# A two-layer attention network: attn3's row sums by quarters of the columns, sums and steps moved, and the last store on another queue

## The chip, the cores and the metric

The kernel runs on one core of one Trainium2 chip. The metric is the device time of one execution in microseconds, taken as the median of several runs. The core has four compute engines with instruction streams of their own: PE (TensorE, matrix products), DVE (VectorE), ACT (ScalarE) and POOL (GpSimd). SP (SyncE) issues most of the transfers.

## The reference

The input x has two images of 512 channels and 64 x 32 positions, that is 2048 tokens each, in f32. Two layers follow one another.

```python
# layer 0: full attention, 8 heads of 64, S = 2048 tokens
attn = softmax(q k^T / 8);  x = x + (attn v) Wout + bout
# layer 1: layer norm, then Nystroem attention with 256 landmarks
qL, kL = means of q, k over groups of 8 tokens
attn1 = softmax(q kL^T)      # 2048 x 256
attn2 = softmax(qL kL^T)     # 256 x 256
attn3 = softmax(qL k^T)      # 256 x 2048
out = attn1 @ (pinv(attn2) @ (attn3 @ v))   # pinv: 6 iterations
out = out + depthwise convolution of v over 33 tokens
t = t + out Wout + bout
# then layer norm, and two matrices, the first from 4-bit indices
t = t + (norm(t) W_lora^T) W^T
```

All of it is computed in f32, and the softmaxes are written without a subtraction of the maximum: exponentials are summed, and the product with the values is multiplied by the reciprocal of the sums.

## The kernel before, in words

Heads are worked on in pairs, with one head in partitions 0 to 63 and the other in 64 to 127. There are four pairs for each of the two images. A path called `fast_path` runs where a bound computed from q and k says that the exponentials are safe; the other path is not taken here.

The program order of PE, DVE, ACT and POOL is the order in which the code issues the instructions. Only the transfers on SP's queue are placed by a scheduler, in one order for that queue; each waits in that order for its own inputs and buffers.

**Layer 0** ends with a loop over four blocks of 512 tokens (L1820 and the lines after it). It weaves three generators: the output projection of the next block (`more_out`), the layer norm of this one (`norm`), and the second layer's projections and Gram products for the pairs of the image done before (`more`). `advance(gens, n)` makes n steps of a list of generators. In the norm, a mean and a variance over the channels are products with a constant matrix (`mean_n` L990 and `var_n` L1006), and the square root on ACT needs a table load (L1008). The projections are `pp` (L1245), copied by ACT (L1248); the landmark softmax `X` is normalised on DVE (L1299), and Gram products `pr` of it (L1313) are copied by ACT (L1320) and stored.

**Layer 1** has a main loop over the list `todo`, the four pairs of image 1 and then those of image 0, named 1_1_0 to 1_0_3. While the pseudo-inverse of pair n is iterated on PE (`pinv`, products pa and pb L1538), hooks fill PE's time with work of its neighbours. The hook `chunk(c)` runs after each of the first five iterations, c = 0 to 4, and `last(i)`, i = 0 to 5, between the products of the sixth, which is applied to the values alone (`wp`, L1513).

- In `chunk(c)`, c below 4, stands a quarter of attn3 of pair n+1: scores (L1367), exponentials (L1376), and the products with v, `attn3_values` (L1388, tensor tiles 128*64). Among them stands a quarter of attn1 of pair n-1: scores (L1595), the addition of the two halves (L1604), values (L1611), then `attn1_sums` (products with ones, L779, tiles 128*32, and an ACT copy L1619) and `attn1_inverse` (reciprocal L1624, and a spread). `attn1_end(c-1)` multiplies on DVE (L1631) and adds on POOL (L1632).
- `spread` (L790) is eight transfers on SP from SBUF to SBUF: the sums were made in 32 partitions for each half of the columns, and the reciprocals are copied to all 64 partitions of the head.
- In `chunk(4)` begins `landmarks_values` of pair n+1 (L1407): row sums `rs3` of attn3 by products with ones (L1412, tiles 128*64, every partition of a head gets the sum), an ACT copy (L1421), a reciprocal (L1422) and the multiply (L1423) on DVE, and the loads of X (L1427). After it comes the depthwise convolution of pair n+1, `cv` (L1465), in four blocks of 512 tokens, each copied by ACT.
- For pairs 1_0_1 and 1_0_2 there is no whole tile for the convolution's result. ACT copies each block into a row (L1477) and SP stores that row to `o_fd` (L1478). `row_of` gives rows from a pool of three buffers, which the spreads of attn1 use too.
- After the convolution, PE transposes M (`tp_M`, L1528), ACT copies it (L1529), and `wp` (L1513) multiplies with it. In `last(1)` the generator of `landmarks_values` goes on: transposes `tp` (L1431), a copy Y (L1433) and the loads of A (L1439).

For the first pair, `second_of_first` does the same steps ahead of the loop, with a unit of projections between each two of them.

**The end.** Image 0 is finished by blocks: output projection, norm, the last product `fp_g` (L1694), and for each 128 channels `rest` (multiply L1683, add L1684, store L1685 on SP). The last 128 channels of the last block are done in two halves of 256 columns.

Of the kernel before, what the change touches and what calls it, by code (L numbers as in the profile page):

```python
# [13 lines left out]
ALU = mybir.AluOpType  # L14
AX = mybir.AxisListType

P = 128
# [3 lines left out]
HEADS, D = 8, 64  # L21
NPAIR = HEADS // 2
TB = 512
NTB = S // TB
NST = S // P
LM, POOL = 256, S // 256
# [627 lines left out]
Q = P // 4  # L654
# [9 lines left out]
def fast_path(  # L664
# [35 lines left out]
    nc = tc.nc  # L700
# [27 lines left out]
    def chunked(ap):  # L728
        return ap.rearrange("(k p) n -> p k n", p=P)
# [40 lines left out]
    csum = const.tile([P, B * NPAIR, 4], F32, name="csum1")  # L770


    def sums_of(rs, acc):


        for h in range(2):
            for j in range(2):
                lo = h * D + j * Q
                nc.tensor.matmul(  # L779
                    rs[lo : lo + Q, :LM], lhsT=ones[:, :Q], rhs=acc[:, h, j * LM : (j + 1) * LM],  # L780
                    start=True, stop=True,
                )

    def spread(dst, few):

        for h in range(2):
            for to in range(2):
                for j in range(2):
                    lo, src = h * D + to * Q, h * D + j * Q
                    nc.sync.dma_start(dst[lo : lo + Q, j * LM : (j + 1) * LM], few[src : src + Q, :])  # L790


    def advance(gens, n=1):
# [420 lines left out]
    class Pair:  # L1214
# [192 lines left out]
        def landmarks_values(self):  # L1407

            rs = bank(f"rs3_{self.name}")
            for j in range(2):  # L1410
                for h in range(2):
                    nc.tensor.matmul(  # L1412
                        rs[h * D : (h + 1) * D, :LM],
                        lhsT=ones,
                        rhs=self.acc3[:, h, j * LM : (j + 1) * LM],
                        start=j == 0,
                        stop=j == 1,
                    )
            rinv = self.acc3[:, 0, :]
            yT = rinv[:, LM:]  # L1420
            nc.scalar.copy(rinv[:, :LM], rs[:, :LM])  # L1421
            nc.vector.reciprocal(rinv[:, :LM], rinv[:, :LM])  # L1422
            nc.vector.tensor_tensor(yT, self.av3[:, :LM], rinv[:, :LM], ALU.mult)  # L1423
            X = exps(f"X2_{self.name}").rearrange("p a b -> p (a b)").rearrange("p (h k n) -> p h k n", h=2, k=2)
            self.X = [X[:, h] for h in range(2)]
            for h in range(2):
                nc.sync.dma_start(self.X[h], X_d[self.b, self.hp, h])  # L1427
            yield
            tp = bank(f"tp_{self.name}")
            for t in range(2):  # L1430
                nc.tensor.transpose(tp[:, t * P : (t + 1) * P], yT[:, t * P : (t + 1) * P], ident)  # L1431
            self.Y = lmpool.tile([P, 2, P], F32, tag="Y", name=f"Y_{self.name}")
            nc.scalar.copy(self.Y, tp[:, :LM].rearrange("p (t n) -> p t n", t=2))  # L1433
            A = zpool.tile([P, 2, 2, LM + 1], F32, tag="Q", name=f"A_{self.name}")
            self.A = [A[:, h] for h in range(2)]
            for h in range(2):
                for t in range(2):
                    cols = slice(t * P, LM)
                    nc.sync.dma_start(self.A[h][:, t, cols], A_d[self.b, self.hp, h][:, t, cols])  # L1439
            yield  # L1440
# [193 lines left out]
    class Finish1:  # L1634
# [42 lines left out]
        def map_units(self, bank_of, parts=1):  # L1677


            def rest(m, fp, cols):  # L1680
                xb, toks = self.xb, slice(self.t * TB + cols.start, self.t * TB + cols.stop)
                y = row_of(f"y_{self.name}_{m}_{cols.start}")[:, cols]
                nc.vector.tensor_tensor(y, fp[:, cols], self.rstd[:, cols], ALU.mult)  # L1683
                nc.vector.tensor_tensor(xb[:, m, cols], y, xb[:, m, cols], ALU.add)  # L1684
                nc.sync.dma_start(chunked(out[self.b])[:, m, toks], xb[:, m, cols])  # L1685

            last = None
            for m in range(KC):
                fp = bank_of(m, f"fp_{self.name}_{m}")
                n = TB // (parts if m == KC - 1 else 1)  # L1690
                for lo in range(0, TB, n):
                    cols = slice(lo, lo + n)
                    for k in range(KC):
                        nc.tensor.matmul(  # L1694
                            fp[:, cols], lhsT=mT[:, k, m * P : (m + 1) * P], rhs=self.xn[:, k, cols],
                            start=k == 0, stop=k == KC - 1,
                        )
                    if last is not None:
                        rest(*last)
                    last = m, fp, cols  # L1700
                yield
            rest(*last)
# [117 lines left out]
    for t in range(NTB):  # L1820
        more_out = [out0(t + 1)] if t + 1 < NTB else []
        advance(more)

        next(norm)
        advance(more_out or more)
        if last is not None:
            next(last)
        advance(more_out or more)
        next(norm)
        advance(more_out, 2)  # L1830
        advance(more, 2)

        next(norm)
        last = norm
        while more_out:
            advance(more_out)
        if t + 1 < NTB:
            norm = norm0(t + 1)
            next(norm)
# [38 lines left out]
    def second_of_first():  # L1878
        pair = todo[0]
        yield from values(0)  # L1880
        yield from pair.attn3()
        landmarks, start, conv = pair.landmarks_values(), pair.start_values(), convolution(0)
        for part in (landmarks, conv, landmarks, start, conv):
            next(part)
            yield
        drain(conv)
        next(start)
        yield
# [41 lines left out]
    for n, pair in enumerate(todo):  # L1930
# [24 lines left out]
        def chunk(c):  # L1955
            nonlocal landmarks
            if before and 0 < c <= n_ones:
                before.attn1_end(c - 1)
            if n == NPAIR and c == 1:

                finish.append(finish1_units(1, [p.o for p in todo[:NPAIR]], early))
            advance(finish)
            if c == NTB:
                if after:
                    landmarks = after.landmarks_values()
                    next(landmarks)
                    drain(convolution(n + 1))
                else:
                    advance(finish, 2)
                return  # L1970
            ones_before = before if c < n_ones else None
            if ones_before:
                if c:
                    before.attn1_scores(c, 0)
                    before.attn1_scores(c, 1)
                before.attn1_add(c)
            if after:
                for s, bank_of in ((2 * c, product_bank), (2 * c + 1, bank)):
                    after.attn3_scores(s, bank_of)
                    after.attn3_add(s)  # L1980
            else:
                advance(finish)
            if ones_before:
                before.attn1_values(c)
            if after:
                after.attn3_values(2 * c)
            else:
                advance(finish)
            if ones_before:
                before.attn1_sums(c)  # L1990
            if after:
                after.attn3_values(2 * c + 1)
            if ones_before:
                before.attn1_inverse(c)
            if n == NPAIR + 2 and c % 2:
                advance(finish)

        def last(i):
            nonlocal start
            if i == 1 and after:  # L2000
                next(landmarks)
                drain(landmarks)
                start = after.start_values()
            if i == 2 and after:
                next(start)
            else:
                advance(vals)
            if i == 3 and after:
                next(start)
            if n_ones < NTB:  # L2010

                if i == 0:
                    before.attn1_scores(n_ones, 0)
                    before.attn1_scores(n_ones, 1)
                    before.attn1_add(n_ones)
                if i == 1:
                    before.attn1_values(n_ones)
                if i == 2:
                    before.attn1_sums(n_ones)
                if i == 3:  # L2020
                    before.attn1_inverse(n_ones)
                if i == 5:
                    before.attn1_end(n_ones)
            if i == 5:
                pair.attn1_scores(0, 0)
                pair.attn1_scores(0, 1)
            advance(finish)
# [162 lines left out]
```

## Time and profile before

| What | us |
| --- | --- |
| median of 3 runs | 2738.82 |
| lowest and highest | 2737.63 and 2741.30 |
| the profiled execution's own time | 2739.02 |
| its span in the profile | 2737.2 |
| PE busy in the span | 2695.4 |
| DVE, ACT, POOL busy | 1631.7, 906.3, 162.0 |

The span is what the profiler records from the first to the last event on the core; the execution's own time is 1.8 us longer. Engines work beside each other, so the busy times don't add up. In a timeline, each line has a start and a length in us, the engine, the line of the code, the operation, the output and input tiles, the shape, and how many instructions were joined in the line; brackets give the idle time before it and what ended that. For PE a shape like 128*64 is the part of the array that an instruction uses, as rows by columns. SPq lines are the issues of transfers on SP's queue, not the transfers. The windows view gives, for each stretch of time, its length, each engine's busy time, the granted clock of PE as a share of the full one, the busy share of the DMA engines and GB/s.

### The profile page before, as it was taken

What the parts mean: (1) busy time and instruction counts of PE and PEld (TensorE: products, weight loads), DVE (VectorE), ACT (ScalarE), POOL (GpSimd) and SP (SyncE); (2) the same over time, 40 slices, a digit from 0 to 9 for tenths busy, and PEclk for the clock granted to TensorE, in tenths of its full rate; (3) what the DMA queues carried; (4) which work ended last, traced back from release to release, by engine and by line L of the source; (5) the groups of instructions that cost most, each with busy time, mean ns of one, the idle gap of its engine ahead of it and who ended that gap; (6) DMA issues with size and microseconds to landing.
All of it is one profiled execution on the core that took longest, in us unless ns stands there. A gap on an engine that the chain in (4) does not pass through costs nothing.

```text
span 2737.2 us, 41174 instructions
## 1 busy us (share of the span) xinstructions
PE 2695.4 (98%) x16994; PEld 1361.0 (50%) x16994; DVE 1631.7 (60%) x2087; ACT 906.3 (33%) x1352; POOL 162.0 (6%) x109
## 2 busy tenths in 40 slices
PE   9999999999999999999999999999999999999999
PEld 5343343434443334344344455777677666655344
DVE  3867777664557765656667544445544645465565
ACT  1434444434334334444422223223323223231210
POOL 0101011000001100000002000000000000000000
PEclk9999999999999999999999999999999999999999
DMA  4100000212111200012024632312211112111211
GB/s 147 41 11 24 24 24 24 86 36 70 32 63 57 97 24 20 24 40 77 24 89 163 209 120 93 103 34 87 81 37 62 59 44 87 44 60 53 89 39 47
DMA packets 111476, 173.99 MB, mean 64 GB/s; under 512 B 16176, under 2 KB 67888, under 8 KB 106672
## 3 DMA queue, kind: packets, MB, share of 16 engines
q1 hardware_dynamic: 105136, 150.00, 16.9%
q0 software_dynamic: 5440, 20.97, 2.1%
q8 instruction: 135, 2.21, 0.3%
q14 instruction: 61, 0.50, 0.1%
q10 hardware_dynamic: 704, 0.31, 0.0%
HBM read 90.87 MB, written 63.57 MB: 56 GB/s over the span
## 4 chain that ended last, share of the span: by engine, by line
PE 91%; DVE 5%; DMA 1%; ACT 1%; SPq 1%; issue 1%; POOL 0%; DVEq 0%; ACTq 0%; POOLq 0%
PE sc_f L1072 15%; PE av_f L1102 15%; PE pp L1245 8%; PE pa L1538 5%; PE pb L1538 5%; PE vp_f L953 4%; PE vp L953 4%; PE pp_k_f L905 4%; PE yp_g L968 4%; PE yp_f L968 4%; PE fp_g L1694 4%; PE pp_q_f L905 3%; PE av L1388 2%; PE sc L1367 2%; PE sc L1595 2%; PE av L1611 2%
## 5 line engine op out<-in xcount | busy, mean ns | idle before, releaser
L1090 DVE TENSOR_TENSOR acc_f<-acc_f,p_f 128x1024 f32<-128x1024 f32 x448 | 581.3, 1297 | 209.9 <-ACT p_f L1080 181.4
L1080 ACT ACTIVATE p_f<-sc_f 128x1024 f32<-128x1024 f32 x512 | 496.7, 1022 | 563.9 <-PE sc_f L1072 561.2
L1072 PE MATMUL sc_f<-q_f,k_f 64*64 64x512 f32 x4096 | 491.1, 594 | 2.7 <-ACT p_f L1080 2.7
L1102 PE MATMUL av_f<-p_f,v_f 64*64 64x512 f32 x4096 | 484.3, 589 | 0.0
L1102 PEld LDWEIGHTS av_f<-p_f,v_f 64*64 64x64 f32 x4096 | 156.5, 133 | 283.0 <-issue 283.0
L1072 PEld LDWEIGHTS sc_f<-q_f,k_f 64*64 64x64 f32 x4096 | 145.8, 133 | 285.6 <-issue 261.9
L1245 PE MATMUL pp<-xh,w 128*128 128x512 f32 x512 | 229.5, 600 | 0.7 <-ACT q L1248 0.7
L1538 PE MATMUL pa<-M 128*128 128x192 f32 (+1 forms) x640 | 153.1, 384 | 6.0 <-ACT M L1529 6.0
L1245 PEld LDWEIGHTS pp<-xh,w 128*128 128x128 f32 x512 | 95.3, 191 | 121.3 <-issue 113.8
L1538 PE MATMUL pb<-R 128*128 128x192 f32 (+1 forms) x640 | 149.3, 380 | 0.0
L1538 PEld LDWEIGHTS pa<-M 128*128 128x128 f32 x640 | 109.3, 195 | 27.6 <-ACT M L1529 9.1
L953 PEld LDWEIGHTS vp_f<-wv_f,x 128*128 128x128 f32 x1024 | 115.7, 192 | 13.5 <-issue 11.8
L953 PE MATMUL vp<-w,xh 128*128 128x128 f32 x1024 | 120.9, 276 | 0.0
L953 PEld LDWEIGHTS vp<-w,xh 128*128 128x128 f32 x1024 | 117.0, 192 | 7.2 <-issue 4.6
L905 PE MATMUL pp_k_f<-x,wk_f 128*128 128x512 f32 x256 | 116.0, 606 | 2.8 <-DVE k_f L908 2.4
L953 PE MATMUL vp_f<-wv_f,x 128*128 128x128 f32 x1024 | 118.7, 277 | 0.0
L1538 PEld LDWEIGHTS pb<-R 128*128 128x128 f32 x640 | 106.5, 190 | 23.2 <-DVE M L1551 0.4
L905 PE MATMUL pp_q_f<-x,wq_f 128*128 128x512 f32 x256 | 114.2, 598 | 0.8 <-DVE q_f L908 0.5
L968 PE MATMUL yp_g<-o,wo_f 128*128 128x512 f32 x256 | 114.8, 597 | 0.0
L968 PE MATMUL yp_f<-q_f,wo_f 128*128 128x512 f32 x256 | 113.5, 598 | 0.8 <-DVE xr_f L975 0.8
L1120 POOL TENSOR_TENSOR q_f<-q_f,rinv_f 128x512 f32<-128x512 f32 x32 | 46.7, 1459 | 1039.3 <-DMA rinv_f<-acc_f 761.1
L1551 DVE SCALAR_TENSOR_TENSOR R<-M,pa 128x320 f32<-128x320 f32 (+1 forms) x160 | 59.9, 416 | 67.8 <-PE pa L1538 67.8
(210 smaller groups left out, 2764.8 us busy)
## 6 DMA issues: line engine op xcount, KB each, us to landing
xh<-xh_fd SPq DMA_DIRECT2D x12, 1024.0 KB, 5.5
rinv_f<-acc_f SPq DMA_DIRECT2D x256, 32.0 KB, 1.9
xr_f<-in_x_dram SPq DMA_DIRECT2D x8, 1024.0 KB, 5.2
x_fd<-xr_f POOLq DMA_DIRECT2D x8, 1024.0 KB, 4.8
xh_fd<-xn_f POOLq DMA_DIRECT2D x8, 1024.0 KB, 4.7
k_fd<-k SPq DMA_DIRECT2D x32, 256.0 KB, 2.9
q_fd<-q SPq DMA_DIRECT2D x32, 256.0 KB, 2.9
k<-k_fd SPq DMA_DIRECT2D x8, 1024.0 KB, 6.6
```

The source lines that it names most:

```text
L905: nc.tensor.matmul(pp, lhsT=w_sb[kind][:, k, cols], rhs=xbs[t][:, k, :], start=k == 0, stop=k == KC - 1)
L953: nc.tensor.matmul(vp[:, j * P : (j + 1) * P], lhsT=xb[:, k, j * P : (j + 1) * P], rhs=w_of(k), start=k == 0, stop=k == KC - 1,)
L968: nc.tensor.matmul(yp, lhsT=wo_sb[:, k, m * P : (m + 1) * P], rhs=oTs[k][:, toks], start=k == 0, stop=k == NPAIR - 1,)
L1072: nc.tensor.matmul(sc[r * D : (r + 1) * D, h, :], lhsT=hd.k[rows, lo : lo + D], rhs=hd.q[rows, t * TB : (t + 1) * TB], start=True, stop=True,)
L1080: nc.scalar.activation(p, sc, AF.Exp, scale=D**-0.5)
L1090: nc.vector.tensor_tensor(acc, first if c == 1 else acc, p, ALU.add)
L1102: nc.tensor.matmul(av[r][half, :], lhsT=hd.v[keys, c, half], rhs=pp[keys, h, :], start=c == 0, stop=c == NST - 1,)
L1245: nc.tensor.matmul(pp, lhsT=self.w[j][:, c, :], rhs=xhs[t][:, c, :], start=c == 0, stop=c == KC - 1)
L1367: nc.tensor.matmul(scs[h][:, j * LM : (j + 1) * LM], lhsT=self.k[rows, c * P : (c + 1) * P], rhs=self.L[0][rows, :], start=True, stop=True,)
L1538: nc.tensor.matmul(dst, lhsT=lhsT[:, k, t * P : (t + 1) * P], rhs=rhs[:, k, :], start=k == 0, stop=k == 1)
L1551: nc.vector.scalar_tensor_tensor(out, m, scale, pr, ALU.mult, ALU.subtract)
L1694: nc.tensor.matmul(fp[:, cols], lhsT=mT[:, k, m * P : (m + 1) * P], rhs=self.xn[:, k, cols], start=k == 0, stop=k == KC - 1,)
```

## The change

It has four parts.

1. Attn3's row sums in `landmarks_values` are made like those of attn1, but for quarters of the columns: 32 columns of ones make the sums of 128 columns in each of four groups of 32 partitions, and the two parts of the exponentials' sum are added up in the product. ACT copies 128x128, DVE takes the reciprocal of 128x128, and eight transfers on SP spread it. The multiply with the values moves behind a new `yield`, into `last(0)`; in `second_of_first` it comes one unit later.
2. `attn1_sums` moves behind the second `attn3_values` of its chunk.
3. In layer 0's last block, where `more_out` is empty, `more` makes four steps instead of two ahead of the norm's next step.
4. The store of the last 256 columns of the final block goes out on ACT's queue.

```diff
-    def sums_of(rs, acc):
-        for h in range(2):
-            for j in range(2):
-                lo = h * D + j * Q
-                nc.tensor.matmul(
-                    rs[lo : lo + Q, :LM], lhsT=ones[:, :Q], rhs=acc[:, h, j * LM : (j + 1) * LM],
-                    start=True, stop=True,
-                )
+    def sums_of(rs, acc, parts=1):
+        n = TB // parts // 2
+        for part in range(parts):
+            for h in range(2):
+                for j in range(2):
+                    lo, at = h * D + j * Q, part * 2 * n + j * n
+                    nc.tensor.matmul(
+                        rs[lo : lo + Q, :n], lhsT=ones[:, :Q], rhs=acc[:, h, at : at + n],
+                        start=part == 0, stop=part == parts - 1,
+                    )
...
     def spread(dst, few):
+        n = few.shape[1]
...
-                    nc.sync.dma_start(dst[lo : lo + Q, j * LM : (j + 1) * LM], few[src : src + Q, :])
+                    nc.sync.dma_start(dst[lo : lo + Q, j * n : (j + 1) * n], few[src : src + Q, :])
...
         def landmarks_values(self):
             rs = bank(f"rs3_{self.name}")
-            for j in range(2):
-                for h in range(2):
-                    nc.tensor.matmul(
-                        rs[h * D : (h + 1) * D, :LM],
-                        lhsT=ones,
-                        rhs=self.acc3[:, h, j * LM : (j + 1) * LM],
-                        start=j == 0,
-                        stop=j == 1,
-                    )
-            rinv = self.acc3[:, 0, :]
-            yT = rinv[:, LM:]
-            nc.scalar.copy(rinv[:, :LM], rs[:, :LM])
-            nc.vector.reciprocal(rinv[:, :LM], rinv[:, :LM])
-            nc.vector.tensor_tensor(yT, self.av3[:, :LM], rinv[:, :LM], ALU.mult)
+            sums_of(rs, self.acc3, 2)
+            few, rinv, yT = self.acc3[:, 0, :P], self.acc3[:, 0, LM:], self.acc3[:, 1, :LM]
+            nc.scalar.copy(few, rs[:, :P])
+            nc.vector.reciprocal(few, few)
+            spread(rinv, few)
...
+            yield
+            nc.vector.tensor_tensor(yT, self.av3[:, :LM], rinv, ALU.mult)
             yield
...
-                nc.sync.dma_start(chunked(out[self.b])[:, m, toks], xb[:, m, cols])
+                queue = nc.scalar if cols.start else nc.sync
+                queue.dma_start(chunked(out[self.b])[:, m, toks], xb[:, m, cols])
...
-        advance(more_out, 2)
-        advance(more, 2)
+        advance(more, 2 if advance(more_out, 2) else 4)
...
-        for part in (landmarks, conv, landmarks, start, conv):
+        for part in (landmarks, conv, landmarks, landmarks, start, conv):
...
-            if ones_before:
-                before.attn1_sums(c)
             if after:
                 after.attn3_values(2 * c + 1)
             if ones_before:
+                before.attn1_sums(c)
                 before.attn1_inverse(c)
...
         def last(i):
             nonlocal start
+            if i == 0 and after:
+                next(landmarks)
```

## The prediction

> **What bounds the kernel now.** I read the page's busy shares first, then its chain of work that ended last, then timelines of the places that the change touches.
>
> ```profile
> span 2737.2 us, 41174 instructions
> ...
> PE 2695.4 (98%) x16994; PEld 1361.0 (50%) x16994; DVE 1631.7 (60%) x2087; ACT 906.3 (33%) x1352; POOL 162.0 (6%) x109
> ...
> PE 91%; DVE 5%; DMA 1%; ACT 1%; SPq 1%; issue 1%; POOL 0%; DVEq 0%; ACTq 0%; POOLq 0%
> ```
>
> TensorE (PE) is busy 98% of the span and carries 91% of the chain. So I count only what shortens PE's own stream and what makes PE wait; a faster copy or store by itself counts nothing. All sums are made against the profiled execution, 2739.02 us, of which the span is 2737.2; the median of the runs shown, 2738.82, lies 0.2 below it.
>
> The first timeline is one chunk of the loop over pairs. Columns: start, length, engine, line, operation, tensor tile (rows*columns of the array), shape. The trace shows each f32 matmul of the code as two.
>
> ```profile
> 1838.06 1.03 PE L1388 MATMUL av<-p,v 128*64 128x256 f32 x8
> 1839.02 0.64 PE L779 MATMUL rs<-acc,ones 128*32 128x256 f32 x8
> 1839.59 1.08 PE L1388 MATMUL av<-p,v 128*64 128x256 f32 x8
> 1840.60 0.33 PE L1528 MATMUL p_pa<-ident,M 128*128 128x128 f32 x1
> ```
>
> To see: the sums of attn1 (128*32) stand between two value products of one tile shape (128*64). From start to start the three take 0.96, 0.57 and 1.01 us. In the single instructions, 256-column rounds of one shape follow at 0.21 us, a round across a change of shape at 0.31, and the first round of a shape lasts 0.26. The next timeline is the row sums of attn3 ahead of a convolution, in a pair that stores its convolution row by row.
>
> ```profile
> 2192.59 1.08 PE L1412 MATMUL rs<-acc,ones 128*64 128x256 f32 x8
> 2194.15 1.75 DVE L1422 RECIPROCAL acc<-acc 128x256 f32<-128x256 f32 x1 [0.70 <-ACT acc L1421]
> 2195.49 2.84 SPq L1478 DMA_DIRECT2D o_fd<-o  x3
> 2198.60 0.59 ACT L1477 COPY o<-cv 128x512 f32<-128x512 f32 x1 [0.61 <-PE cv L1465]
> 2198.80 1.41 PE L1513 MATMUL wp<-M 128*64 128x256 f32 x8
> 2199.08 0.44 ACT L1529 COPY M<-tp_M 128x128 f32<-128x128 f32 x2
> ```
>
> To see: three stores leave as soon as their rows are copied; the fourth row's copy starts 6.01 us after the sums, and behind it on ACT stand the copies of M that the second half of the wp product needs (PE's weight load at 2199.40 is released by them). The pair's reciprocal ends 3.31 us after the sums' start. Last, the issue of one spread, and the norm step at the end of layer 0:
>
> ```profile
> 2450.79 4.95 SPq L790 DMA_DIRECT2D rinv<-acc  x8
> ```
>
> ```profile
> 1497.00 1.48 PE L1006 MATMUL var_n<-xr_f,mean_w 128*128 128x512 f32 x2 [3.68 <-issue]
> ...
> 1498.28 4.95 PE L1245 MATMUL pp<-xh,w 128*128 128x512 f32 x8
> ```
>
> ```profile
> core 0: us, PE busy (x) PEld busy (x) DVE busy (x) ACT busy (x) POOL busy (x), PEclk, DMA share, GB/s
> 1493.20:1497.00 3.80, 0.12 (x1) 0.03 (x1) 3.77 (x9) 0.86 (x2) 1.36 (x2) 1.00 0.53 195
> 1497.60:1501.00 3.40, 3.40 (x6) 1.34 (x5) 3.23 (x7) 1.97 (x2) 0.00 (x0) 0.50 0.50 181
> 2437.80:2440.20 2.40, 0.34 (x3) 0.00 (x1) 2.37 (x6) 0.00 (x0) 0.00 (x0) 1.00 0.44 125
> 2440.20:2443.60 3.40, 3.40 (x26) 1.90 (x27) 0.14 (x1) 1.36 (x4) 0.00 (x0) 1.00 0.00 0
> ```
>
> To see, in the windows: after an idle stretch of 3.8 us PE had half its clock for 3.4 us; after one of 2.4 it kept the full clock.
>
> **What the Trainium skill says.** *TensorEngine Tiling (Array Packing)*, Key Properties: changing the tiling mode, not just the tile, drains TensorE. The trace agrees: 0.31 against 0.21 us. *TensorE: Matmul & The Clock Gate*, Part 1: a free-running window of 3413 ns watches PE, and one idle window halves its clock. The trace agrees with half clock for 3.41 us after 3.85 idle; since the window is free-running, an idle of little over 3.4 us need not fill one. *DMA: Bandwidth & Descriptors*, Anatomy of one DMA: waits are made by the issuing sequencer before it dispatches; so a transfer issued late is late whole, however idle the DMA engines are. The trace shows 1.9 us from issue to landing for a spread, 2.2 to 3.0 for these 256 KB stores. *Trainium Kernel Development and Optimization*, Key Constraints: issuing from several engines saves only the sequencers' issue time.
>
> **The change, part by part.**
>
> *attn1's sums behind the second value product.* Nothing is added; two 128*64 groups become neighbours. The three groups and the first flip behind them take 1.89 us now, start to start; with one change of shape fewer, and its slow first round, 1.74. So 0.15 us in each of 23 places: **−3.5**. The reciprocal and spread of these sums come later against PE by one product, 0.86 us; the av bank they free is asked for by the next attn1 values 2.2 to 3.5 us later in most chunks and 1.1 at least. Cover enough, so 0; if it were gone the loss would be some 0.3 us in the tightest chunks, 2 in all.
>
> *attn3's sums by quarters.* Before, from the sums to the convolution 0.92 us (1797.44 to 1798.35). After: eight 32-column matmuls of 128 columns in four rounds. The trace has no such rounds; halving the 256-column ones gives 0.14, 0.11, 0.11 and 0.20 with the change of shape, about 0.56, and 0.05 more in the convolution's first round. Bounds: nothing gained, if 16 weight loads of some 0.11 us set the pace, to 0.36. I take 0.30 in the loop's pairs and 0.44 in the first, which a projection of a third shape follows anyhow. In two of the seven loop pairs a stall (below) swallows it, so 5 x 0.30 + 0.44: **−1.9**. A copy (0.37 to 0.27) and a reciprocal (1.75 to about 0.95) get shorter; neither ends a wait of PE.
>
> *The spread that follows.* Eight issues on SP, 0.62 us each, start 2.0 us after the sums (0.63 matmuls, 0.27 copy, 1.0 reciprocal) and hold SP until +7.0; it lands by +8.3 to +10. The multiply and the transposes wait for that: PE comes to the transposes at about +11.1 in most pairs and at +9.5 in the last, multiply done by +10.6 and +9.2. Hidden, except the third pair, where SP is late with the spread before (0.3 taken, up to 0.6), and the first pair of all, whose sums stand at 1687.50: there the reciprocal waits for VectorE until 1692.7, the spread lands about 1699.9, the multiply ends about 1700.4, and PE is there at about 1699.0: 1.5 (0 to 1.9). Together **+1.8**.
>
> *What SP's queue is moved past.* Behind the spread on SP stand the row stores of pairs 1_0_1 and 1_0_2. The rows have three buffers, so the fourth copy needs the first store landed. Before: issued +2.90, landed +5.89 and +5.08, copy at +6.01: free. After: issued +7.0, landed +9.2 to +10.0, so the copy starts 3.2 to 4.0 us late, the copies of M behind it as well, and PE, which had resumed with the second half of wp at +6.47, resumes 0.81 to 0.84 after the copy, at +10.1 to +10.9. That is 3.6 to 4.4 us later than before, all of it on the path, and PE, which arrives 0.3 earlier, is idle for that much more. I take 3.8 in each of two pairs: **+7.6**. The five other pairs of the loop keep their convolution in a whole tile and wait for no store.
>
> *Half clock after it.* An idle of about 4.1 us (3.8 and the 0.3) is at the edge. I let one of the two be followed by 3.4 us at half clock, which does 1.7 us of work: **+1.7**; bounds 0 and 3.4.
>
> *The norm step.* One projection (of k, 3.4 us) and two Gram products go ahead of var_n, into the 3.7 us before 1497.00 in which PE did nothing. Bound above: that idle time and the half clock after it, together up to 3.5 of gain after what stays; but the first Gram product waits for the normalised X at 1498.44, so var_n moves to about 1500.2, and the second pair of Gram products waits on ACT for the table load (1.28) and square root behind var_n. Following PE to the next q projection, 1506.16 before, I reach 1503.7: **−2.4** (0.7 to 3.5).
>
> *The last store on ACT.* It leaves 0.02 us after the last VectorE add ends, at 2732.77, and SP was waiting for that, not busy. ACT is idle then. **0**, ±0.4.
>
> Sum: −3.5 − 1.9 + 1.8 + 7.6 + 1.7 − 2.4 + 0 = **+3.3**. Profiled 2742.3; median 2742.1. About 0.2%, 5.5 us, is what a measurement of this kernel can tell from no change. This case alone spans 2738.5 to 2745.5.
>
> **The rivals.**
>
> A: the stores are not held, because SP takes the stores first or the spread's issues are hidden. Against: the instruction order on SP puts the spread ahead, and an issue of eight took 4.95 us. Then −3.5 − 2.5 (the sums' gain counts in all pairs) + 1.8 − 2.4 = −6.6 remain: 2732.2. It asks for no wait in the two pairs.
>
> B, slower: the store's landing, not its issue, decides. If it lands 3.0 us after issue (as one did before), the loss is 4.4 or more, past the 3.85 us that was seen to halve the clock. With 4.5 us lost and 1.7 at half clock in both pairs, it is +12.4 instead of +9.3: +6.4, or 2745.2; with the quarters' gain at its lower bound too (weight loads) 1.9 more, 2747.1. I take 2745.8. The deciding point is an idle time over 3.85 us in both. For it: the four half-clock stretches of the trace follow long idles. Against: two idles of just such length are needed.
>
> C: the rows of the new spread are half as long (512 bytes), and its issues take half the time. Then o_fd leaves at about +4.8 and PE resumes some 1.8 us later than before in each pair, without half clock: −6.6 + 0.6 + 3.6 = −2.4, or 2736.4. Against: the 256 KB stores issue in 0.32 us, so issue time doesn't follow bytes.
>
> That the change doesn't do what it says (32-column rounds no faster) is +1.9, inside the forecast's own range.
>
> **How the numbers follow.** Main case 0.46, A 0.11, B 0.30, C 0.13. The range holds the main case, C and nearly all of B: 2734 to 2748. Faster by 0.2% needs under 2733.3: most of A, 0.09. Slower needs over 2744.3: nearly all of B and the main case's edge, 0.32. Within: 0.59.
>
> **What would show it.** In the profile after: the wp product waiting on ACT's copy of M for about 3.8 us in two pairs, with o_fd issued behind eight acc transfers; nothing ahead of var_n but pp and pr; two value products of attn3 in one row of x16; a row 128x128 for the sums; half clock once or twice behind the convolutions. Wrong if o_fd is issued before +5 us, if the chunks keep their length, or if PE stalls at the transposes in the loop's pairs.

## The result, and the profile after

| Kernel | median, us | runs | ratio to the kernel before, 95% interval |
| --- | --- | --- | --- |
| before, measured beside it | 2738.54 | 13 | |
| after | 2744.48 | 13 | 1.0022 (1.0015 to 1.0030) |

The changed kernel is 5.9 us slower, inside the range and 2.4 us over the predicted 2742.1. The profiled execution took 2744.41 us against 2739.02 before; its span is 2742.6 against 2737.2, 5.4 us longer.

From the page of the kernel after, the span and the busy times:

```profile
span 2742.6 us, 41416 instructions
...
PE 2691.6 (98%) x17058; PEld 1364.5 (50%) x17058; DVE 1624.6 (59%) x2087; ACT 902.7 (33%) x1352; POOL 163.7 (6%) x109
```

PE was busy 3.8 us less than before, though more of it at half clock, and not busy for 51.0 us in place of 41.8: the products got cheaper, and PE stood still for more than that. PE's waits, from the answer for the kernel after (who waits, for whom, us in total, times, longest):

```profile
PE wp L1510 <- ACT o L1474: 5.1, 1, 5.1
PE wp L1510 <- ACT M L1526: 4.0, 1, 4.0
...
PE pr L1317 <- DVE X L1303: 1.8, 1, 1.8
...
PE pr L1317 <- ACT rstd_n L1012: 1.2, 1, 1.2
```

Two waits of wp, 5.1 and 4.0 us, are new; before, wp waited 0.4 for a row copy. Ahead of var_n nothing waits any more; 1.8 and 1.2 us stand there instead, for X and for the square root. The timeline of pair 1_0_1, which answers to the one shown of before:

```profile
2187.90 0.64 PE L782 MATMUL rs<-acc,ones 128*32 128x128 f32 x16
2188.96 0.95 DVE L1417 RECIPROCAL acc<-acc 128x128 f32<-128x128 f32 x1 [0.20 <-ACT acc L1416]
2189.97 4.95 SPq L794 DMA_DIRECT2D acc<-acc  x8
2195.02 1.50 SPq L1475 DMA_DIRECT2D o_fd<-o  x3
2197.67 0.59 ACT L1474 COPY o<-cv 128x512 f32<-128x512 f32 x1 [4.65 <-DMA o_fd<-o]
2198.15 0.44 ACT L1526 COPY M<-tp_M 128x128 f32<-128x128 f32 x2
2198.47 0.82 PE L1510 MATMUL wp<-M 128*64 128x256 f32 x4 [3.99 <-ACT M L1526]
```

Read it downwards, with times counted from the start of the sums at 2187.90: the spread is issued from +2.1 to +7.0, the first row store at +7.1, its landing releases the fourth row's copy at +9.8 (ACT had waited 4.65 us), the copy of M follows, and PE resumes at +10.6 after 3.99 us idle. In pair 1_0_2 the same chain is longer:

```profile
2311.73 5.78 SPq L794 DMA_DIRECT2D acc<-acc  x8
...
2317.61 1.72 SPq L1475 DMA_DIRECT2D o_fd<-o  x3
...
2320.16 0.58 ACT L1474 COPY o<-cv 128x512 f32<-128x512 f32 x1 [5.44 <-DMA o_fd<-o]
...
2320.80 1.98 PE L1510 MATMUL wp<-M 128*64 128x256 f32 x8 [5.15 <-ACT o L1474]
```

The eight issues took 5.78 us here, and PE waited 5.15. Windows of the two idle stretches and of what follows them:

```profile
2194.50:2198.45 3.95, 0.00 (x0) 0.00 (x0) 0.42 (x1) 0.78 (x3) 0.00 (x0) 1.00 0.65 220
2199.60:2202.90 3.30, 3.30 (x17) 3.30 (x17) 0.00 (x0) 0.10 (x1) 0.00 (x0) 0.50 0.85 200
2315.70:2320.75 5.05, 0.00 (x0) 0.00 (x0) 0.42 (x1) 0.59 (x2) 0.00 (x0) 0.83 0.50 168
2320.80:2325.80 5.00, 5.00 (x22) 3.87 (x23) 1.38 (x2) 0.65 (x3) 0.00 (x0) 0.50 0.44 140
```

PE's clock (the third number from the end) is 0.50 after both. To see where the 5.4 us come from, I took the start of each product in both traces and followed the difference, after minus before. This table is called the ladder below.

| Stretch | change of the difference, us |
| --- | --- |
| up to the norm step (layer 0, which the change leaves alone) | −1.2 |
| norm step of layer 0's last block | −2.3 |
| first pair: sums, spread, transposes | +1.3 |
| attn1's sums, 23 places at −0.153 | −3.5 |
| attn3's sums in the four loop pairs where the gain stays | −1.3 |
| third pair of the loop (1_1_3): sums and a wait for the spread | +0.8 |
| pairs 1_0_1 and 1_0_2, idle time: 3.76 and 4.49 | +8.3 |
| the same, half clock: 1.63 and 2.38 | +4.0 |
| start of pair 1_0_3's inverse | −1.2 |
| elsewhere | +0.1 |
| last product to the end of the span | +0.4 |

A ladder compares two single executions. Up to the norm step, all ten other profiles are 0.5 to 2.6 us ahead of the one of the kernel before, whatever they change; so the first row says nothing about the change.

### The profile page after: what moved, and what is told of

It reads as the page before. It is cut to its first block, busy times and chain, and to the rows that moved or that the text cites. A ratio compares the mean times of both kernels' runs of the same rounds, so it can differ in the third digit from the quotient of the medians.

```text
span 2742.6 us, 41416 instructions
## 1 busy us (share of the span) xinstructions
PE 2691.6 (98%) x17058; PEld 1364.5 (50%) x17058; DVE 1624.6 (59%) x2087; ACT 902.7 (33%) x1352; POOL 163.7 (6%) x109
## 4 chain that ended last, share of the span: by engine, by line
PE 90%; DVE 5%; DMA 1%; ACT 1%; SPq 1%; issue 1%; POOL 0%; DVEq 0%; ACTq 0%; POOLq 0%
PE sc_f L1076 15%; PE av_f L1106 15%; PE pp L1249 7%; PE pa L1535 5%; PE pb L1535 5%; PE vp_f L957 4%; PE vp L957 4%; PE pp_k_f L909 4%; PE fp_g L1693 4%; PE pp_q_f L909 4%; PE yp_g L972 4%; PE yp_f L972 4%; PE sc L1592 2%; PE sc L1371 2%; PE av L1392 2%; PE av L1608 2%
## 5 line engine op out<-in xcount | busy, mean ns | idle before, releaser
L1693 PE MATMUL fp_g<-xn_g,mT 128*128 128x512 f32 (+1 forms) x232 | 99.8, 580 | 0.0
```

Of the source, the lines that this page charges most:

```text
L1693: nc.tensor.matmul(fp[:, cols], lhsT=mT[:, k, m * P : (m + 1) * P], rhs=self.xn[:, k, cols], start=k == 0, stop=k == KC - 1,)
```

## The experiments

All are timed beside the kernel before, whose median lay between 2738.14 and 2738.34 there.

**The row stores on another queue.**

```diff
-                    nc.sync.dma_start(o_d[self.b, self.hp][:, toks], row)
+                    nc.gpsimd.dma_start(o_d[self.b, self.hp][:, toks], row)
```

> The changed kernel with one edit: the row stores of pairs 1_0_1 and 1_0_2 are issued on POOL's queue, no longer behind the eight transfers of the spread on SP. Theory (the place on SP's queue makes the two stalls of 4.0 and 5.1 us and the half clock after them, some 12 us of the changed kernel): the first store leaves about 3 us after the sums, the fourth copy is free or late by under 1 us, and the time is 2731 to 2735, below the kernel before (2738.5). Rival (the stores land late because the spread's transfers are in flight beside them): the wait on the store stays over 3 us, and the time is over 2741.

Measured: 2732.16 us, ratio 0.9976 (0.9967 to 0.9986). From its timeline in pair 1_0_1:

```profile
2189.30 4.95 SPq L794 DMA_DIRECT2D acc<-acc  x8
2190.11 0.59 POOL L1475 DMA_DIRECT2D o_fd<-o  x1 [2.85 <-ACT o L1474]
...
2192.95 0.58 ACT L1474 COPY o<-cv 128x512 f32<-128x512 f32 x1 [0.61 <-PE cv L1462]
```

The spread is still there and takes as long; the store no longer stands behind it, and the fourth copy waits for the convolution alone. In pair 1_0_2 PE still waits 0.86 us. One word moved gives back 12.3 us of the changed kernel. This makes SP's order the cause, and the rival is out as the main cause. A trace of it remains: in pair 1_0_2 the first store landed 3.2 us after its issue, against 2.6 in the median.

**Half of the spread in two pairs.**

```diff
-    def spread(dst, few):
+    def spread(dst, few, tos=(0, 1)):
...
-            for to in range(2):
+            for to in tos:
...
-            spread(rinv, few)
+            spread(rinv, few, (0,) if self.name in ("1_0_1", "1_0_2") else (0, 1))
```

> The changed kernel, but the spread of attn3's reciprocals in pairs 1_0_1 and 1_0_2 alone has four transfers in place of eight; half of the rows of those two pairs keep numbers that are not reciprocals, which leaves out part of the computation and none of the other work. Theory (issue time on SP decides): the first store leaves 2.5 us earlier, the stalls are about 1.5 and 2.3 us in place of 4.0 and 5.1, neither is followed by half clock, and the time is 2735 to 2738. Rival (one late landing or one semaphore decides, whatever the number of issues): both stalls stay over 3.5 us, 2743 to 2745. Second rival (half clock follows any idle stretch of more than 1 us in this place): stalls shorter, half clock stays, 2738 to 2741.

Measured: 2734.72 us, ratio 0.9988 (0.9981 to 0.9994), 0.3 us under the expected range. From its timeline in pair 1_0_2:

```profile
2307.46 3.04 SPq L794 DMA_DIRECT2D acc<-acc  x4
2310.59 1.50 SPq L1475 DMA_DIRECT2D o_fd<-o  x3
2313.11 0.58 ACT L1474 COPY o<-cv 128x512 f32<-128x512 f32 x1 [2.66 <-DMA o_fd<-o]
...
2313.74 1.08 PE L1510 MATMUL wp<-M 128*64 128x256 f32 x8 [2.37 <-ACT o L1474]
```

Four issues fewer, 2.74 us less of issuing, and the wait of PE there falls from 5.15 to 2.37 us. The wait follows the issues about one for one, and the store stayed on SP here, so that the first experiment's other queue is not what did it. In pair 1_0_1 it falls from 3.99 to 1.46. No half clock follows either. Of the 9.8 us that this kernel is faster than the changed one, 5.3 are the idle time of the two pairs and 4.0 the half clock behind it.

**Each part alone.** The diffs are the parts of the change as shown above, each put into the kernel before; in the second of the five runs the first part alone is taken out of the changed kernel.

> The kernel before with the first part of the change alone (row sums of attn3 by quarters, their spread, the multiply one step later). Theory (this part carries the whole loss: two stalls with half clock 12, first pair 1.1 net, third pair 1.0, five sums gained 0.3 each): 11 to 13 us over the kernel before, about 2750. Rival (the loss comes from the moved sums of attn1, whose spread goes on SP a microsecond later): at most 3 us over the kernel before, 2741.

Measured: 2749.19 us, ratio 1.0036 (1.0022 to 1.0049), 10.9 us slower than before: the one part that loses. The waits of wp are there (4.8 and 4.0 us) without the moved sums, so these don't make them.

> The changed kernel without the first part: attn1's sums moved, the norm step moved, the last store on ACT. Theory: -3.5 for the sums, -2.1 for the norm, +0.4 for the store: 5 us below the kernel before, about 2733.3 (2732 to 2735). Rival (the moved sums make the stalls): 2741 or more.

Measured: 2732.04 us, ratio 0.9976 (0.9968 to 0.9984), 6.3 us faster than before.

> The kernel before with the second part alone: attn1's sums behind the second product with v of attn3, 23 places. Theory: 0.15 us saved in each place and nothing else changed, -3.5 us, about 2734.9 (2734 to 2736); in the trace the second group of value products follows the first at the pace of one tile shape. Rival (the later spread delays attn1's ends and the saving is given back): within 1 us of the kernel before.

Measured: 2735.16 us, ratio 0.9988 (0.9980 to 0.9996), 3.0 faster. The chunk that was shown of before, in the kernel after:

```profile
1835.55 1.90 PE L1392 MATMUL av<-p,v 128*64 128x256 f32 x16
1837.38 0.64 PE L782 MATMUL rs<-acc,ones 128*32 128x256 f32 x8
1837.95 0.33 PE L1525 MATMUL p_pa<-ident,M 128*128 128x128 f32 x1
```

Both value groups are one row of x16, 1.83 us to the sums, and 0.57 more to the transpose of M (`p_pa`, the prediction's flip): 2.40 for what took 2.54 (1838.06 to 1840.60).

> The kernel before with the third part alone, the two steps more ahead of the last norm's variance. Theory: the wait of 3.7 us ahead of var_n and the half clock after it go, waits of 1.9 us for the normalised X and 1.2 us for the square root come in their place, -2.1 us, about 2736.3. Rival (a later place on the path gives it back, since ACT's copies and the norm's end come later): no difference, 2738.3.

Measured: 2735.75 us, ratio 0.9992 (0.9985 to 0.9998), 2.4 faster.

> The kernel before with the fourth part alone, the last store on ACT's queue. Theory: no gain, and at the span's end some 0.4 us more from the last product to the end of the span (6.9 us in place of 6.5, as in the profile of the changed kernel). Rival (the 0.4 us was the noise of one landing): 6.5 us again. The time can't tell these apart, the profile's end can: 2738 to 2739 in both.

Measured: 2738.31 us, ratio 1.0002 (0.9993 to 1.0010). From the last product to the span's end it has 6.8 us, between the two theories. Over all eleven profiles, the five with that store on ACT have 6.7 to 7.5, the six with it on SP 6.5 to 8.4. So the 0.4 us in the ladder is within what a landing varies by, and the queue makes no difference that these runs show.

The parts add up: −3.0 − 2.4 + 0.2 + 10.9 = +5.7, with 5.9 measured for all together. Without the quarters, the other three should then give −5.2, and −6.3 was measured; that difference lies within the intervals.

**Versions without the wait.** In the first, quarters in six pairs and the row stores on POOL. In the second, quarters in four pairs (`quarters = self.name in ("1_1_1", "1_1_2", "1_0_0", "1_0_3")`) and the row stores on SP. Both have the last store on SP. The diff is that of the first, without its store lines and without the products of the other branch, which are those of the kernel before.

```diff
+            quarters = self.name not in ("1_1_0", "1_1_3")
...
+            if quarters:
                 sums_of(rs, self.acc3, 2)
...
                 spread(rinv, few)
+            else:
...
+                nc.scalar.copy(rinv, rs[:, :LM])
+                nc.vector.reciprocal(rinv, rinv)
+                nc.vector.tensor_tensor(yT, self.av3[:, :LM], rinv, ALU.mult)
```

> The changed kernel with the row stores of two pairs on POOL's queue, the last store back on SP, and the sums by quarters left out in the first pair and in 1_1_3, whose transposes waited for the spread. Theory: all gains without the waits that took them: -3.5 for attn1's sums, -2.1 for the norm, -0.3 in each of six pairs, together 7.4 below the kernel before, about 2731 (2729.5 to 2732.5), the fastest of all. Rival (the store queue's change costs as much as the quarters gain): 2732 to 2733, no better than without the quarters.

Measured: 2731.18 us, ratio 0.9972 (0.9961 to 0.9982). The time is as expected, yet in pair 1_0_2 a store issued by POOL landed only after 4.2 us, PE waited 1.78, and half clock followed. Its interval overlaps with that of the kernel without quarters, so the two are not told apart.

> The changed kernel with the sums by quarters kept only in the four pairs whose transposes and stores did not wait for the spread (1_1_1, 1_1_2, 1_0_0, 1_0_3), the sums as before in the other four, the row stores on SP as before and the last store on SP. Theory: -3.5 for attn1's sums, -2.1 for the norm, -0.3 in each of four pairs, and no new wait: 6.8 below the kernel before, about 2731.3 (2730 to 2732.5), with no wait of the row copies over 0.7 us. Rival (a spread on SP costs something in every pair): no better than the changed kernel without the quarters, 2732 to 2733.

Measured: 2729.34 us, ratio 0.9969 (0.9958 to 0.9981), the lowest time of all, 9.0 below the kernel before. No row copy waits for a store. It is 2.2 better than expected. Its interval, 6 us wide, overlaps with that of the kernel without quarters, so a gain from the quarters in these four pairs is not shown.

Its profile has two things that were not expected. The start of pair 1_0_3's inverse comes 1.2 us sooner, as in all six kernels with the quarters in that pair; in the four others it moves by −0.4 to +0.2. In the kernel before, PE waits 1.00 us there for DVE, which had waited for attn1's last spread: its multiply began 2.80 us after that spread's issues ended. In the changed kernel it began 1.57 us after them, and PE's wait is gone. Why that spread lands sooner is not shown. Against this stands a stretch of half clock from 2432.02 that costs 1.2 us, so these two don't explain the 2.2.

## Why the prediction was right, and where it was off

*attn1's sums, −3.5.* Right: 0.153 us in each place in the trace, and 3.0 in the time of that part alone. No given-back delay is seen. The 1.89 us named there start with the last round of the first value group; all three groups take the 2.54 us above. The saving of 0.15 doesn't change by that.

*attn3's sums by quarters, −0.30 each.* Right. From the sums to the convolution it is 0.57 us in place of 0.92, and the ladder has 0.28 to 0.29 in three pairs and 0.41 in the last. The weight loads didn't set the pace.

*First pair, +1.5 − 0.44.* Right: +1.25 in all where 1.06 was forecast, with PE idle 1.50 us ahead of the transposes.

*Third pair, +0.3.* Undersized, past its bound of 0.6: 1.1 in the ladder, beside −0.3 for the sums. PE waited 0.88 us for the multiply, because the spread's eight issues took 5.95 us there, not 4.95. I had priced all spreads at one row's duration, though in the trace of the kernel before 16 of the 64 spreads took 5.3 to 6.1 us.

*The stalls, +7.6.* The mechanism was right step by step: order on SP, landing, row copy, copy of M, wp. The size was 8.3. Pair 1_0_1 came in at 3.76 against 3.8. Pair 1_0_2 came in at 4.49, since its eight issues took 5.78 us. The fourth copies started 2.65 and 2.55 us after the first store's issue, within the 2.2 to 3.0 stated for the landing. One reading was off: in pair 1_0_1 PE resumed with the second half of wp at +6.81 (2199.40), not +6.47, so the forecast resumption meant 3.3 to 4.1 us later than before; the measured 3.76 lies in both ranges.

*Half clock, +1.7.* This is the term that was mis-sized most: 4.0, because it followed both stalls, and the second for two stretches of 3.41 us, 2.38 us lost. I let one of two be hit since an idle of 4.1 seemed only little longer than the 3.41 us window. That reasoning was wrong (see the last section), and the trace of the kernel before spoke against it. PE's idle time ahead of 1497.00 is 3.68 us in it, not 3.85. The first of its four half-clock stretches, at 33.26, follows only 2.40 us idle, so not all four follow long ones. The 2.40 us at 2437.80 that kept the full clock hold 2.06 us idle.

*The sum.* With what these four terms were short of, 0.2 for the first pair, 0.8 for the third, 0.7 for the stalls and 2.3 for the half clock, the forecast goes from +3.3 to +7.3. The ladder has +5.4, mainly since two rows that no term of the prediction names go the other way: −1.2 in layer 0, and −1.2 at pair 1_0_3's inverse. So that the predicted time came within 2.4 us is in part luck; the mechanism was right.

*The norm step, −2.4.* Right: −2.3 in the ladder, −2.4 by the time of that part alone, with the two waits where they were expected: for X, and for the square root.

*The last store, 0.* Right.

*The rivals.* A and C are out: the stores were held, and eight issues with half the bytes took as long as before or longer. The time falls just past the point where I let B begin (2744.3). B's deciding point was met, both idle times over 3.85 us and half clock after both, but not by B's price: the landing was not 3.0 us; the issue was longer, in one pair.

## What to carry to other kernels

A transfer that is added to a queue in program order costs its issue time to whatever stands behind it: eight small transfers at 0.62 to 0.74 us each held a store by 5 to 6 us, and the store held a buffer, an ACT copy and PE in turn. Before adding a spread, list what is issued behind it and when those buffers are needed next; keep the gain only in the places where nothing is. Price a stall with the clock that follows it: of the 12.3 us here, a third was half clock.

## What the runs showed of the hardware

The Trainium skill's page *TensorE: Matmul & The Clock Gate*, Part 1, says that PE falls to half clock after at least one idle window of some 3.4 us. The length agrees with these traces, but a window need not be idle throughout. The half-clock stretches of one trace begin on a grid of 3.4133 us: in the changed kernel at 15.02, 2199.55, 2319.01, 2530.64 and 2738.85, the last four 640, 675, 737 and 798 steps after the first. So I summed PE's idle time in each window of that grid, in eleven traces. All 34 windows at full clock with 1.94 us or more idle were followed by half clock. Between 1.78 and 1.89 us one was and four were not. Of 122 windows with 1.0 to 1.77 us idle none was. One stretch, in the kernel without the quarters, began after a window with only 0.94 us idle, and I can't explain it.

In pair 1_0_1 the window that ended at 2199.55 had 2.34 us idle. With half the spread, the 2.37 us of pair 1_0_2 fell in two windows, 1.11 and 1.26, and the clock stayed full. The clearest case is a wait of 2.06 us that `wp` has for DVE's R in every trace, ahead of pair 1_0_3's inverse. In ten traces the grid cuts it, with at most 1.67 us in one window, and the clock stays full. In the version with quarters in four pairs it lies whole in one window, and half clock follows. Where the grid lies differs from execution to execution. On these counts, an idle time of 4 us has at least 2 us in one window wherever the grid lies, and it should have been priced as certain.

The issue of eight small transfers from SBUF to SBUF took 4.95 us in most places and up to 6.3 in others, in all eleven traces; what lengthens it was not tried.
